# A two-layer MetaFormer on one core: the middle channel group laid out in alternating rows, and the next step's pieces at other places in the loop

## The chip, the core and the metric

The kernel runs on one core of a Trainium2 chip. The core has a matrix engine (TensorE, PE in the profile), a vector engine (VectorE, DVE), an activation engine (ScalarE, ACT), a general engine (GpSimd, POOL) and a queue that issues DMAs (SyncE, SP). Each engine works through its own list of instructions in order; semaphores tie the lists together. The metric is the time of one launch in microseconds; the kernel before took 13006.98 us, the median of three runs (13003.53 to 13008.28).

## What is computed

The input is two images of 96 channels, 128 by 128. Layer 0 is a four-direction selective scan (Mamba) and a feed-forward block, layer 1 a 3x3 convolution and a feed-forward block. Nearly all the time goes into the scan. Cut to that:

```python
def _mamba(x, in_w, conv_w, conv_b, xproj_w, dt_w, dt_b, A_log, Dp, outp_w):
    xc, z = jnp.split(x @ in_w.T, 2, axis=-1)                   # 192 channels each
    xc = silu(causal_conv(xc, conv_w, taps=4) + conv_b)
    xdbl = xc @ xproj_w.T
    dt_raw, Bm, Cm = xdbl[..., :6], xdbl[..., 6:22], xdbl[..., 22:]   # 16 states
    dt = softplus(dt_raw @ dt_w.T + dt_b)
    A = -exp(A_log)
    h = 0
    for t in range(L):                                          # L = 16384
        h = exp(dt[t, :, None] * A) * h + dt[t, :, None] * Bm[t] * xc[t, :, None]
        y[t] = (h * Cm[t]).sum(-1)
    return ((y + Dp * xc) * silu(z)) @ outp_w.T
```

It runs in four directions (rows, rows reversed, columns, columns reversed); the four results are joined, multiplied by `fuse_w` and added to the input.

## The kernel before

For each image, `normalize` writes the normalised image to DRAM by rows (`xnr`) and by columns (`xnc`), `mamba` does the scan, and `ffn_and_conv` the rest.

`mamba` takes the directions in two pairs, rows with columns, then both reversed. A pair has 2 x 192 = 384 channels, held as three groups of 128 partitions: group 0 is channels 0 to 127 of the first direction, group 2 is channels 64 to 191 of the second, and the middle group is mixed: its lower 64 partitions are channels 128 to 191 of the first direction and its upper 64 are channels 0 to 63 of the second. The time axis is cut into 32 tiles of T = 512, which makes 64 steps for an image, 128 in all.

A step has 24 units: 3 groups x 8 pairs of states. A loop turn k is one unit, and its main instructions are:

- POOL, `b_part` (L324): the row of B, spread over the partitions, times dt·u; two units ahead.
- ACT, `decay` (L330): two activations write exp(dt·A) into the PSUM tile `da`, of which there are three; two units ahead.
- DVE, `scan` (L334): two scans, one for each state, in place in `da`.
- In `behind`, one unit later: DVE multiplies the states by the row of C (L409), ACT copies the last column to `hst` (L410), and PE adds the two products into `y` by an identity matmul (`sums`, L341). At a group's end, which comes up in turn 1, 9 and 17 of a step, DVE multiplies y by the gate (`gated`, L349), and PE opens the next y with the `dmat` matmul (L416). There is one buffer for y.

The rows of B and C reach the partitions through DRAM. `rows_out` copies the 64 rows of a step to SBUF and writes them to the DRAM tile `bcd`, in four copies and by four DMAs (L261). `row_tile` (L320) reads a quad of states back, broadcast over the partitions: one DMA for groups 0 and 2, and for the middle group one for each 64 partitions, since the two halves belong to different directions. The buffers hold four quads of B and three of C; a C buffer is free when PE's `sums` has read it.

Everything of the next step that comes before its scan is cut into pieces and laid between the units of the running step (`prologue`; the list `at`). Each entry is (turn, where, piece); where = 0 comes at the start of a turn, before the scans, and where = 1 at its end, after `feed_decay`. The pieces are `load` (xa, xb), the `conv` of each group (the four taps folded into the weights, PE, L207) and its `conv_out` (ACT, L233), `gate` (PE, L207) and `gate_out` (ACT, L241), two `silu` over all three groups with an activation table load on either side (L244, L245), `rows`, and for each group the chain dt_in to dt_u (PE, ACT, POOL). Their PSUM results, and that of the output projection `project`/`collect` (L357 to L365, laid 4 turns behind a group's end), share the single buffer `misc`. The program order is the order on each engine:

```python
                issue(k, 0)
                ...
                    scan(i, g, s, 0, da, b, hs[k])
                if 0 < k <= total:
                    behind(k - 1)
                ...
                feed_decay(k + AHEAD)
                issue(k, 1)
```

In the middle group, `inproj` issues two matmuls for each tap: 64 output columns from xa to the lower half of the PSUM tile, 64 from xb to the upper half.

Of the kernel before, what the change touches and what calls it, by code (L numbers as in the profile page):

```python
# [10 lines left out]
F32 = mybir.dt.float32  # L11
# [4 lines left out]
ALU = mybir.AluOpType  # L16
# [16 lines left out]
COPIES = 4  # L33
# [4 lines left out]
BCO = 32  # L38
NBC = 4 * S
# [3 lines left out]
def tile_metaformer(ctx: ExitStack, tc: tile.TileContext, a: dict, out: bass.AP):  # L43
    nc = tc.nc

    cpool = ctx.enter_context(tc.tile_pool(name="const", bufs=1))
# [19 lines left out]
    inz = const("inz", (C, 4, DI))  # L66
# [11 lines left out]
    inx = cpool.tile([C, 4, 4, DI], F32, name="inx")  # L78
    nc.vector.memset(gmat, 0.0)
    with tc.tile_pool(name="prep", bufs=1) as pp, tc.tile_pool(name="prep_ps", bufs=2, space=PSUM) as pps:  # L80
        alog = pp.tile([128, 2, NG, S], F32, name="alog")
        nc.sync.dma_start(alog, a["alog"])
        nc.scalar.activation(alog, alog, AF.Exp)
        nc.vector.tensor_scalar_mul(amat, alog, -1.0)

        dskip = pp.tile([128, 2, NG], F32, name="dskip")
        nc.sync.dma_start(dskip, a["dskip"])
        for pi in range(2):
            for g in range(NG):
                nc.vector.tensor_scalar_mul(dmat[:, pi, g, :], ident, dskip[:, pi, g : g + 1])  # L90

        inxw = pp.tile([C, 4, DI], F32, name="inxw")
        nc.sync.dma_start(inxw, a["inx"])
        taps = pp.tile([C, 4, 4, DI], F32, name="taps")
        nc.sync.dma_start(taps, a["taps"].broadcast_to((C, 4, 4, DI)))
        for d in range(4):
            nc.vector.tensor_tensor(inx[:, d], taps[:, d], inxw[:, d, None, :].broadcast_to((C, 4, DI)), ALU.mult)
        outw = pp.tile([C, 4, DI], F32, name="outw")
        nc.sync.dma_start(outw, a["outw"])
        fusew = pp.tile([C, 4, C], F32, name="fusew")  # L100
        nc.sync.dma_start(fusew, a["fusew"])
        for pi, (da, db) in enumerate(PAIRS):

            pieces = [
                (slice(0, 128), da, 0, 128),
                (slice(0, 64), da, 128, 192),
                (slice(64, 128), db, 0, 64),
                (slice(0, 128), db, 64, 192),
            ]
            for g, (rows, d, lo, hi) in enumerate(pieces):  # L110
                ps = pps.tile([128, C], F32, name="ps")
                nc.tensor.matmul(ps[rows, :], outw[:, d, lo:hi], fusew[:, d, :], start=True, stop=True)
                nc.vector.tensor_copy(gmat[rows, pi, g, :], ps[rows, :])

    def layernorm(x, eps, dst, wp, psp, bufs=2, **cast):

# [66 lines left out]
    def mamba(acc, xnr, xnc):  # L183

        with ExitStack() as st:
# [3 lines left out]
            rows_d = pool("rows_d", 3, space=DRAM)  # L189
# [4 lines left out]
            def misc():  # L194
                return ps_m.tile([128, T], F32, name="misc")

            def inproj(pi, g, w, src, taps):

                ps = misc()
                for k in taps:  # L200
                    se = {"start": k == taps[0], "stop": k == taps[-1]}
                    for d, rows, lo, hi in (
                        ((0, slice(0, 128), 0, 128),),
                        ((0, slice(0, 64), 128, 192), (1, slice(64, 128), 0, 64)),
                        ((1, slice(0, 128), 64, 192),),
                    )[g]:
                        nc.tensor.matmul(ps[rows, :], w(PAIRS[pi][d], k, lo, hi), src[d][:, k : k + T], **se)  # L207
                return ps

            def prologue(pi, i, d):  # L210

                rev = pi == 1
                lo = L - (i + 1) * T if rev else i * T
                src = []
# [10 lines left out]
                    d["dt"], d["dtu"], d["yg"] = [], [], []  # L225

                def conv(g):
                    d["ps"] = inproj(pi, g, lambda dd, k, lo, hi: inx[:, dd, k, lo:hi], src, (0, 1, 2, 3))

                def conv_out(g):  # L230
                    if g == 0:
# [1 line left out]
                    nc.scalar.activation(d["xc"][:, g, :], d["ps"], AF.Identity, bias=convb[:, pi, g : g + 1])  # L233

                def gate(g):
                    d["ps"] = inproj(pi, g, lambda dd, k, lo, hi: inz[:, dd, lo:hi], src, (3,))

                def gate_out(g):
                    if g == 0:
# [82 lines left out]

            def b_part(d, g, b):
# [242 lines left out]
def _layout(v):  # L566

    f = np.float32
    order = [d for pair in PAIRS for d in pair]
    rows = lambda w: w[order].reshape(2, NG, 128, -1).transpose(2, 0, 1, 3)  # L570
# [11 lines left out]
    grouped = lambda w: w.reshape(2, NG, 128, -1).transpose(2, 0, 1, 3)  # L582
    out = {
        "x": v["x"].reshape(NB, C, L),
        "ident": np.eye(128, dtype=f),
        "inx": v["L0_conv_in_w"][:, :DI].transpose(2, 0, 1),
        "inz": v["L0_conv_in_w"][:, DI:].transpose(2, 0, 1),
        "taps": v["L0_conv_conv_w"].transpose(0, 2, 1)[None],
        "convb": rows(v["L0_conv_conv_b"])[..., 0],
        "bcw": grouped(bcw),  # L590
        "dtw": dtw,
        "dtb": rows(v["L0_conv_dt_b"])[..., 0],
        "alog": rows(v["L0_conv_A_log"]),
        "dskip": rows(v["L0_conv_Dp"])[..., 0],
        "outw": v["L0_conv_outp_w"].transpose(1, 0, 2),
        "fusew": v["L0_conv_fuse_w"].reshape(C, 4, C).transpose(2, 1, 0),
        "fuseb": v["L0_conv_fuse_b"].reshape(C, 1),
        "kw": v["L1_conv_kernel"].transpose(1, 2, 3, 0).reshape(C, 9, C),
    }
# [23 lines left out]
```

## Time and profile before

| What | us |
|---|---|
| median of the runs | 13006.98 |
| the profiled execution, its run | 13004.29 |
| its span | 13002.5 |
| DVE busy in it | 11569.1 |
| of that, scans (L334) | 7339.4 |
| of that, products with C (L409) | 3705.9 |
| PE busy, as modelled | 10850.3 |
| POOL busy | 9215.4 |
| ACT busy | 8560.0 |

A line of a timeline reads: start, duration, engine, line, operation, output<-inputs with their shapes, the number of instructions merged into it, and in brackets the idle time before it with what ended that. A line of the waits reads: engine, tile and line that waited, what it waited for, then the total in us, the number of times and the longest. An engine may stand idle at no cost if it isn't the one that sets the pace, so a wait counts where it delays the engine that does.

### The profile page before, as it was taken

What the parts mean: (1) busy time and instruction counts of PE and PEld (TensorE: products, weight loads), DVE (VectorE), ACT (ScalarE), POOL (GpSimd) and SP (SyncE); (2) the same over time, 40 slices, a digit from 0 to 9 for tenths busy, and PEclk for the clock granted to TensorE, in tenths of its full rate; (3) what the DMA queues carried; (4) which work ended last, traced back from release to release, by engine and by line L of the source; (5) the groups of instructions that cost most, each with busy time, mean ns of one, the idle gap of its engine ahead of it and who ended that gap; (6) DMA issues with size and microseconds to landing.
All of it is one profiled execution on the core that took longest, in us unless ns stands there. A gap on an engine that the chain in (4) does not pass through costs nothing. (4 is left out here: it accounts for less than half of the span.)

```text
span 13002.5 us, 97992 instructions
## 1 busy us (share of the span) xinstructions
PE 10850.3 (83%) x24208; PEld 3987.1 (31%) x24208; DVE 11569.1 (89%) x10865; ACT 8560.0 (66%) x14738; POOL 9215.4 (71%) x4772
## 2 busy tenths in 40 slices
PE   6888888888888888888978888888888888888889
PEld 2323233333333333333323333332333333333233
DVE  5999999999999999995459999999999999999954
ACT  6666666666666666665566666666666666666655
POOL 4877778777787787772147778777787777877721
PEclk8999999999999999999989999999999999999999
DMA  7999999999999999992079999999999999999920
GB/s 226 287 294 282 298 288 285 295 283 298 288 285 295 283 295 289 285 295 68 13 226 285 298 283 292 290 285 298 285 291 291 284 298 286 290 294 281 296 61 13
DMA packets 545331, 3400.40 MB, mean 262 GB/s; under 512 B 81612, under 2 KB 82732, under 8 KB 146840
## 3 DMA queue, kind: packets, MB, share of 16 engines
q1 hardware_dynamic: 544760, 3394.12, 83.1%
q8 instruction: 195, 3.19, 0.1%
q14 instruction: 376, 3.08, 0.1%
HBM read 3288.94 MB, written 104.86 MB: 261 GB/s over the span
## 5 line engine op out<-in xcount | busy, mean ns | idle before, releaser
L324 POOL TENSOR_TENSOR row<-dtu,row 128x1024 f32<-128x1024 f32 x3072 | 7175.7, 2358 | 1739.3 <-DMA row<-bcd 1419.2
L334 DVE TENSOR_TENSOR_SCAN da<-da,hst,row 128x512 f32<-128x512 f32 x5952 | 7339.4, 1274 | 351.2 <-ACT da L330 194.6
L341 PE MATMUL y<-row,ident 128*128 128x512 f32 x12288 | 6120.1, 626 | 1113.3 <-DVE row L409 1098.9
L330 ACT ACTIVATE da<-dt,amat 128x512 f32<-128x512 f32 x6144 | 4249.4, 692 | 207.5 <-ACT hst L410 0.4
L341 PEld LDWEIGHTS y<-row,ident 128*128 128x128 f32 x12288 | 2288.9, 197 | 4779.4 <-DVE row L409 2292.3
L409 DVE TENSOR_TENSOR row<-da,row 128x1024 f32<-128x1024 f32 x3072 | 3705.9, 1206 | 19.6 <-DMA row<-bcd 18.8
L410 ACT COPY hst<-da 128x2 f32<-128x2 f32 x3072 | 484.0, 158 | 2235.5 <-DVE row L409 2233.3
L416 PE MATMUL y<-xc,dmat 128*128 128x512 f32 x768 | 526.1, 773 | 779.1 <-DVE sz L349 779.1
L287 POOL TENSOR_TENSOR q<-e,q 128x512 f32<-128x512 f32 x384 | 488.0, 1271 | 821.8 <-ACT hst L410 709.1
L233 ACT ACTIVATE xc<-misc,convb 128x512 f32<-128x512 f32 x384 | 264.2, 688 | 1117.5 <-PE misc L207 1117.5
L207 PE MATMUL misc<-xa,inx 96*128 96x512 f32 (+1 forms) x2048 | 932.4, 597 | 59.0 <-DMA xa<-xnr 57.2
L207 PE MATMUL misc<-xb,inx 96*64 96x512 f32 (+1 forms) x2048 | 928.1, 595 | 1.6 <-ACT xc L233 1.6
L531 POOL TENSOR_TENSOR acc<-acc,y 96x512 f32<-96x512 f32 x128 | 147.6, 1153 | 987.0 <-DVE y L530 987.0
L541 PE MATMUL pc<-pad,kw 96*96 96x512 f32 x1152 | 566.7, 593 | 0.0
L207 PEld LDWEIGHTS misc<-xa,inx 96*128 96x128 f32 (+1 forms) x2048 | 323.6, 163 | 625.5 <-issue 493.4
L293 POOL TENSOR_TENSOR dt<-dt,ln 128x512 f32<-128x512 f32 x384 | 486.9, 1268 | 30.1
L297 POOL TENSOR_TENSOR dtu<-dt,xc 128x512 f32<-128x512 f32 x384 | 488.5, 1272 | 0.5
L290 POOL TENSOR_TENSOR ln<-ln,q 128x512 f32<-128x512 f32 x384 | 488.1, 1271 | 0.5
L359 PE MATMUL misc<-sz,gmat 128*96 128x512 f32 x1024 | 483.6, 594 | 0.0
L416 PEld LDWEIGHTS y<-xc,dmat 128*128 128x128 f32 x768 | 129.0, 211 | 1102.1 <-DVE sz L349 1099.1
L268 PE MATMUL misc<-rows,dtw 12*128 12x512 f32 x768 | 439.7, 652 | 18.5 <-ACT dt L275 17.2
L132 DVE TENSOR_TENSOR xq<-xm,rs 96x512 fp8e5<-96x512 f32 x128 | 87.9, 687 | 387.8 <-ACT rs L128 387.8
(75 smaller groups left out, 8403.8 us busy)
## 6 DMA issues: line engine op xcount, KB each, us to landing
row<-bcd SPq DMA_DIRECT2D x2048, 1024.0 KB, 7.5
row<-bcd SPq DMA_DIRECT2D x2048, 512.0 KB, 8.0
bcd<-rows SPq DMA_DIRECT2D x512, 128.0 KB, 9.8
xa<-xnr SPq DMA_DIRECT2D x124, 193.1 KB, 5.8
xb<-xnc SPq DMA_DIRECT2D x124, 193.1 KB, 5.5
acc<-in_x_dram SPq DMA_DIRECT2D x16, 768.0 KB, 17.8
xnr<-xn SPq DMA_DIRECT2D x16, 768.0 KB, 4.3
xnc<-stg SPq DMA_DIRECT2D x16, 768.0 KB, 5.6
```

Source lines behind the costliest of these rows:

```text
L207: nc.tensor.matmul(ps[rows, :], w(PAIRS[pi][d], k, lo, hi), src[d][:, k : k + T], **se)
L287: nc.gpsimd.tensor_tensor(d["q"], d["e"], d["q"], ALU.subtract)
L290: nc.gpsimd.tensor_tensor(d["ln"], d["ln"], d["q"], ALU.add)
L293: nc.gpsimd.tensor_tensor(d["dt"][g], d["dt"][g], d["ln"], ALU.add)
L297: nc.gpsimd.tensor_tensor(dtu, d["dt"][g], d["xc"][:, g, :], ALU.mult)
L324: nc.gpsimd.tensor_tensor(b, d["dtu"][g][:, None, :].broadcast_to((128, 2, T)), b, ALU.mult)
L330: nc.scalar.activation(da[:, j, :], d["dt"][g], AF.Exp, scale=amat[:, pi, g, s + j : s + j + 1])
L334: nc.vector.tensor_tensor_scan(h[:, j, :], da[:, j, :], b[:, j, :], 0.0 if i == 0 else hst[:, g, s + j : s + j + 1], ALU.mult, ALU.add,)
L341: nc.tensor.matmul(y, ident, c[:, j, :], start=False, stop=s + j == S - 1)
L409: nc.vector.tensor_tensor(c, h, c, ALU.mult)
L416: nc.tensor.matmul(y, dmat[:, pi, g, :], d["xc"][:, g, :], start=True, stop=False)
L541: nc.tensor.matmul(pc, kw[:, t, :], rows, start=t == 0, stop=t == 8)
```

## The change

The channels of the middle group are put in turn: even partitions hold the first direction, odd partitions the second. The weights are laid out on the host for this, with zeros in the rows (columns of the stationary operand) that belong to the other direction, so that every matmul of the middle group fills all 128 partitions: for each tap one from xa and one from xb are added into the same PSUM tile. `bcd` is written as two DMAs (B and C), each of which writes all four copies, and a quad of rows for the middle group is read by one DMA over all partitions, like those of the other groups. The order of the channels in `convb`, `bcw`, `dtw`, `dtb`, `alog`, `dskip` follows (`perm`). At the start, the taps are multiplied in one tap at a time through one buffer. The pieces of the next step stand at other turns.

```diff
-        taps = pp.tile([C, 4, 4, DI], F32, name="taps")
-        nc.sync.dma_start(taps, a["taps"].broadcast_to((C, 4, 4, DI)))
-        for d in range(4):
-            nc.vector.tensor_tensor(inx[:, d], taps[:, d], inxw[:, d, None, :].broadcast_to((C, 4, DI)), ALU.mult)
...
+        for k in range(4):
+            taps = pp.tile([C, 2, NG + 1, 128], F32, name="taps")
+            nc.sync.dma_start(taps, a["taps"][:, k].broadcast_to((C, 2, NG + 1, 128)))
+            nc.vector.tensor_tensor(inx[:, k], taps, inxw, ALU.mult)
...
-            def inproj(pi, g, w, src, taps):
+            def inproj(g, w, src, taps):
 
                 ps = misc()
-                for k in taps:
-                    se = {"start": k == taps[0], "stop": k == taps[-1]}
-                    for d, rows, lo, hi in (
-                        ((0, slice(0, 128), 0, 128),),
-                        ((0, slice(0, 64), 128, 192), (1, slice(64, 128), 0, 64)),
-                        ((1, slice(0, 128), 64, 192),),
-                    )[g]:
-                        nc.tensor.matmul(ps[rows, :], w(PAIRS[pi][d], k, lo, hi), src[d][:, k : k + T], **se)
+                parts = [(k, j) for k in taps for j in ((0,), (1, 2), (3,))[g]]
+                for n, (k, j) in enumerate(parts):
+                    nc.tensor.matmul(ps, w(k, j), src[j // 2][:, k : k + T], start=n == 0, stop=n == len(parts) - 1)
                 return ps
...
                 def rows_out():
-
                     d["rows"] = one.tile([BCO + NBC, T], F32, name="rows")
                     nc.scalar.copy(d["rows"], d["ps"][0 : BCO + NBC, :])
-                    d["bcd"] = rows_d.tile([COPIES, 2, NBC // 2, T], F32, name="bcd")
-                    for n in range(COPIES):
-                        nc.sync.dma_start(d["bcd"][n].rearrange("k r t -> (k r) t"), d["rows"][BCO:, :])
+
+                def rows_to_dram():
+
+                    d["bcd"] = rows_d.tile([2, COPIES, NBC // 2, T], F32, name="bcd")
+                    for k in range(2):
+                        r = d["rows"][BCO + k * NBC // 2 : BCO + (k + 1) * NBC // 2, None, :]
+                        r = r.broadcast_to((NBC // 2, COPIES, T))
+                        nc.sync.dma_start(d["bcd"][k].rearrange("n r t -> r n t"), r)
...
-                at = [(0, 0, load), (8, 1, partial(silu, "xc")), (14, 1, partial(silu, "sz"))]
-                at += [(12, 0, rows), (12, 1, rows_out)]
-                for g, k in enumerate((4, 5, 6)):
-                    at += [(k, 0, partial(conv, g)), (k, 1, partial(conv_out, g))]
-                for g, k in enumerate((7, 10, 11)):
-                    at += [(k, 0, partial(gate, g)), (k, 1, partial(gate_out, g))]
-                for g, k in enumerate((13, 18, 21)):
-                    pieces = (0, 0, dt_in), (0, 1, dt_exp), (1, 1, dt_ln), (2, 0, dt_q), (3, 0, dt_log), (3, 0, dt_sum), (4, 0, dt_u)
+                at = [(0, 0, load), (7, 1, partial(silu, "xc")), (12, 1, partial(silu, "sz"))]
+                at += [(12, 1, rows), (13, 0, rows_out), (13, 1, rows_to_dram)]
+                for g, k in enumerate((2, 4, 6)):
+                    at += [(k, 0, partial(conv, g)), (k + 1, 0, partial(conv_out, g))]
+                for g, k in enumerate((9, 10, 11)):
+                    at += [(k, 1, partial(gate, g)), (k + 1, 0, partial(gate_out, g))]
+                for g, k in enumerate((14, 17, 20)):
+                    pieces = (0, 1, dt_in), (1, 0, dt_exp), (1, 1, dt_ln), (3, 0, dt_q), (4, 0, dt_log), (4, 0, dt_sum), (5, 0, dt_u)
                     at += [(k + m, where, partial(f, g)) for m, where, f in pieces]
...
             def row_tile(d, g, s, k, ahead):
 
                 t = gen.tile([128, 4, T], F32, name=f"row{k}", bufs=ahead + 1)
-                for half in range(2) if g == 1 else (slice(None),):
-                    rows = slice(half * 64, half * 64 + 64) if g == 1 else half
-                    at = s + S * (half if g == 1 else g // 2)
-                    n = (64 if g == 1 else 128) // COPIES
-                    src = d["bcd"][None, :, k, at : at + 4, :].broadcast_to((n, COPIES, 4, T))
-                    nc.sync.dma_start(t[rows], src)
+
+                rows, nd = d["bcd"][k].rearrange("n (d s) t -> n d s t", d=2)[:, :, s : s + 4, :], 2
+                if g != 1:
+                    rows, nd = rows[:, g // 2 : g // 2 + 1], 1
+                src = rows.rearrange("n d s t -> (n d) s t")[None].broadcast_to((128 // nd // COPIES, nd * COPIES, 4, T))
+                nc.sync.dma_start(t, src)
                 return t
...
+    def padded(w):
+
+        t = np.zeros((w.shape[0], 2, NG + 1, 128), f)
+        for pi, (p, q) in enumerate(PAIRS):
+            t[:, pi, 0] = w[:, p, :128]
+            t[:, pi, 1, 0::2] = w[:, p, 128:]
+            t[:, pi, 2, 1::2] = w[:, q, :64]
+            t[:, pi, 3] = w[:, q, 64:]
+        return t
+
```

More of the change, by code (lines that the diff above doesn't have):

```diff
@@ L65, in tile_metaformer @@
     nc.vector.tensor_scalar_add(center, ident[0:C, 0:C], -1.0 / C)
-    inz = const("inz", (C, 4, DI))
+    inz = const("inz", (C, 2, NG + 1, 128))
     convb = const("convb", (128, 2, NG))
@@ L77, in tile_metaformer @@
     gmat = cpool.tile([128, 2, NG + 1, C], F32, name="gmat")
-    inx = cpool.tile([C, 4, 4, DI], F32, name="inx")
-    nc.vector.memset(gmat, 0.0)
+    inx = cpool.tile([C, 4, 2, NG + 1, 128], F32, name="inx")
     with tc.tile_pool(name="prep", bufs=1) as pp, tc.tile_pool(name="prep_ps", bufs=2, space=PSUM) as pps:
@@ L90, in tile_metaformer @@
                 nc.vector.tensor_scalar_mul(dmat[:, pi, g, :], ident, dskip[:, pi, g : g + 1])
-        inxw = pp.tile([C, 4, DI], F32, name="inxw")
+        inxw = pp.tile([C, 2, NG + 1, 128], F32, name="inxw")
         nc.sync.dma_start(inxw, a["inx"])
-        taps = pp.tile([C, 4, 4, DI], F32, name="taps")
-        nc.sync.dma_start(taps, a["taps"].broadcast_to((C, 4, 4, DI)))
-        for d in range(4):
-            nc.vector.tensor_tensor(inx[:, d], taps[:, d], inxw[:, d, None, :].broadcast_to((C, 4, DI)), ALU.mult)
-        outw = pp.tile([C, 4, DI], F32, name="outw")
-        nc.sync.dma_start(outw, a["outw"])
+        for k in range(4):
+            taps = pp.tile([C, 2, NG + 1, 128], F32, name="taps")
+            nc.sync.dma_start(taps, a["taps"][:, k].broadcast_to((C, 2, NG + 1, 128)))
+            nc.vector.tensor_tensor(inx[:, k], taps, inxw, ALU.mult)
+        outx = pp.tile([C, 2, NG + 1, 128], F32, name="outx")
+        nc.sync.dma_start(outx, a["outx"])
         fusew = pp.tile([C, 4, C], F32, name="fusew")
         nc.sync.dma_start(fusew, a["fusew"])
[L102 to L110, printed above, removed]
+        for pi, pair in enumerate(PAIRS):
+            for g in range(NG + 1):
                 ps = pps.tile([128, C], F32, name="ps")
-                nc.tensor.matmul(ps[rows, :], outw[:, d, lo:hi], fusew[:, d, :], start=True, stop=True)
-                nc.vector.tensor_copy(gmat[rows, pi, g, :], ps[rows, :])
+                nc.tensor.matmul(ps, outx[:, pi, g, :], fusew[:, pair[g // 2], :], start=True, stop=True)
+                nc.vector.tensor_copy(gmat[:, pi, g, :], ps)
     def layernorm(x, eps, dst, wp, psp, bufs=2, **cast):
@@ L227, in conv @@
                 def conv(g):
-                    d["ps"] = inproj(pi, g, lambda dd, k, lo, hi: inx[:, dd, k, lo:hi], src, (0, 1, 2, 3))
+                    d["ps"] = inproj(g, lambda k, j: inx[:, k, pi, j, :], src, (0, 1, 2, 3))
                 def conv_out(g):
@@ L235, in gate @@
                 def gate(g):
-                    d["ps"] = inproj(pi, g, lambda dd, k, lo, hi: inz[:, dd, lo:hi], src, (3,))
+                    d["ps"] = inproj(g, lambda k, j: inz[:, pi, j, :], src, (3,))
                 def gate_out(g):
@@ L569, in _layout @@
     order = [d for pair in PAIRS for d in pair]
-    rows = lambda w: w[order].reshape(2, NG, 128, -1).transpose(2, 0, 1, 3)
+    perm = np.arange(2 * DI)
+    perm[128:256] = perm[128:256].reshape(2, 64).T.reshape(-1)
+    grouped = lambda w: w.reshape(2, NG, 128, -1).transpose(2, 0, 1, 3)
+    rows = lambda w: grouped(w[order].reshape(2, 2 * DI, -1)[:, perm])
     xw = v["L0_conv_xproj_w"]
@@ L581, in _layout @@
             dtw[k * RK : (k + 1) * RK, pi, at] = v["L0_conv_dt_w"][d].T
-    grouped = lambda w: w.reshape(2, NG, 128, -1).transpose(2, 0, 1, 3)
+    def padded(w):
[6 more added lines that the diff above has]
+        return t
     out = {
@@ L585, in _layout @@
         "ident": np.eye(128, dtype=f),
-        "inx": v["L0_conv_in_w"][:, :DI].transpose(2, 0, 1),
-        "inz": v["L0_conv_in_w"][:, DI:].transpose(2, 0, 1),
-        "taps": v["L0_conv_conv_w"].transpose(0, 2, 1)[None],
+        "inx": padded(v["L0_conv_in_w"][:, :DI].transpose(2, 0, 1)),
+        "inz": padded(v["L0_conv_in_w"][:, DI:].transpose(2, 0, 1)),
+        "taps": padded(v["L0_conv_conv_w"].transpose(2, 0, 1))[None],
         "convb": rows(v["L0_conv_conv_b"])[..., 0],
-        "bcw": grouped(bcw),
-        "dtw": dtw,
+        "bcw": grouped(bcw[:, perm]),
+        "dtw": dtw[:, :, perm],
         "dtb": rows(v["L0_conv_dt_b"])[..., 0],
@@ L594, in _layout @@
         "dskip": rows(v["L0_conv_Dp"])[..., 0],
-        "outw": v["L0_conv_outp_w"].transpose(1, 0, 2),
+        "outx": padded(v["L0_conv_outp_w"].transpose(1, 0, 2)),
         "fusew": v["L0_conv_fuse_w"].reshape(C, 4, C).transpose(2, 1, 0),
```

## The prediction

> **What bounds the kernel now.** I read the page's busy times first, then who waited for whom in the scan stage of the first image (300 to 6000 us), then the timeline of one step, engine by engine.
>
> ```profile
> PE 10850.3 (83%) x24208; PEld 3987.1 (31%) x24208; DVE 11569.1 (89%) x10865; ACT 8560.0 (66%) x14738; POOL 9215.4 (71%) x4772
> ...
> DMA  7999999999999999992079999999999999999920
> ...
> row<-bcd SPq DMA_DIRECT2D x2048, 1024.0 KB, 7.5
> row<-bcd SPq DMA_DIRECT2D x2048, 512.0 KB, 8.0
> ```
>
> DVE leads, and the DMA engines look full. The last two lines say that half a quad of rows takes as long to land as a whole one. But who waits for it?
>
> ```profile
> POOL row L324 <- DMA row<-bcd: 702.6, 162, 7.1
> ...
> DVE da L334 <- ACT da L330: 98.1, 61, 1.9
> DVE sz L349 <- PE y L341: 82.8, 62, 2.1
> ...
> DVE da L334 <- ACT hst L410: 68.9, 60, 1.6
> ...
> DVE row L409 <- DMA row<-bcd: 9.2, 13, 2.1
> ```
>
> POOL waits for rows; DVE hardly does (9 us in 62 steps). DVE's waits come about once a step each, from ACT and PE. One step of 24 units in DVE's timeline: L349 runs at 1973.19, 2005.49, 2035.37 and 2063.86, so the groups take 32.3, 29.9 and 28.5 us. The third has no idle row and is the floor: 8 units of 3.487 us plus 0.6 for L349. Over all steps the first group takes 31.5 (69 times) or 32.3 (55 times), the others the same; the mean step is 31.86 + 29.9 + 28.5 = 90.26, of which 4.8 us is waiting. All 128 steps together wait some 610 us (4.7%), and that is all the change can win there.
>
> Where the first wait comes from:
>
> ```profile
> 1990.42 0.64 PE L207 MATMUL misc<-xa,inx 96*64 96x512 f32 x1
> 1990.43 0.64 PE L207 MATMUL misc<-xb,inx 96*64 96x512 f32 x1
> 1990.90 0.59 PE L207 MATMUL misc<-xa,inx 96*64 96x512 f32 x1
> 1990.91 0.59 PE L207 MATMUL misc<-xb,inx 96*64 96x512 f32 x1
> ...
> 1995.83 3.60 PE L207 MATMUL misc<-xb,inx 96*128 96x512 f32 x8
> ```
>
> ```profile
> 1999.47 0.69 ACT L233 ACTIVATE xc<-misc,convb 128x512 f32<-128x512 f32 x1 [3.16 <-PE misc L207]
> 2000.06 0.15 ACT L410 COPY hst<-da 128x2 f32<-128x2 f32 x1
> 2000.24 1.41 ACT L330 ACTIVATE da<-dt,amat 128x512 f32<-128x512 f32 x2
> ```
>
> ```profile
> 2001.76 1.29 DVE L334 TENSOR_TENSOR_SCAN da<-da,hst,row 128x512 f32<-128x512 f32 x1 [1.75 <-ACT da L330]
> 2002.96 1.21 DVE L409 TENSOR_TENSOR row<-da,row 128x1024 f32<-128x1024 f32 x1
> 2005.49 0.69 DVE L349 TENSOR_TENSOR sz<-y,sz 128x512 f32<-128x512 f32 x1 [1.33 <-PE y L341]
> ```
>
> The three convs crowd PE, conv_out stands in ACT's order waiting for them, and hst and da behind it come late; the scan starts 0.11 us after da ends. From conv_out's start to the scan is 2.29 us. Note the pairs: in the middle group the xa and xb matmuls, 64 columns each, start 0.01 us apart, so 16 passes take the time of 8 (a float32 matmul is two passes, 0.43 us apart).
>
> The rates and the PE clock (columns: stretch, busy times, then clock, DMA share, GB/s):
>
> ```profile
> 1994.00:2020.00 26.00, 24.93 (x59) 9.58 (x58) 22.51 (x20) 17.97 (x30) 13.00 (x6) 1.00 0.95 223
> 2020.00:2060.00 40.00, 29.26 (x58) 10.26 (x58) 38.84 (x35) 32.05 (x55) 32.99 (x18) 0.96 0.95 352
> ```
>
> ```profile
> 1974.00:1977.00 3.00, 3.00 (x5) 0.70 0.97 309
> ...
> 2064.50:2067.50 3.00, 2.84 (x6) 1.00 0.92 341
> ```
>
> At the same DMA share the half transfers get 223 GB/s, the whole ones 352. The last two lines open two successive steps: one has PE at a reduced clock, the other not; that is the 32.3 against the 31.5.
>
> [...]
>
> **The change part by part.**
>
> *Row DMAs.* 8 fewer issues a step (0.53 us each on SP) and the middle group at the full rate: 8 MB a step at 352 instead of 223 GB/s, 24 instead of 38 us. POOL's 11 us a step of waiting mostly goes. DVE gains only its own DMA waits, 18.8 us in all, and those sat in front of the ACT wait that follows: I take 0. bcd is written by two DMAs instead of four, the same bytes; on SP it now waits for rows_out behind the silu of sz, and the B fetch of unit 14 stands behind it; it is issued by then, took 9.8 us to land and is read at unit 18, 14 us later: 0. Next late on that path: nothing.
>
> *Full-width conv and gate of the middle group.* The pairs are gone: conv(1) is 16 passes in a row, 6.88 us instead of 3.44; gate(1) 1.72 instead of 0.86. PE has 4.3 us more a step in all; on average there is room (PE issues 156 passes, 67 us of 90), but not in the first group.
>
> *The pieces' new units.* As queue order: (k, after the decays) and (k+1, before them) are neighbours on ACT, so conv_out still comes directly behind da of its conv's unit + 2. conv moves from units 4,5,6 to 2,4,6; the silu of xc one unit earlier, 7; the gates to 10,11,12 on PE; the silu of sz from 14 to 12, away from dt_ln. I walk the first group with a full PE clock, time 0 at the L349 that opens it. DVE undisturbed starts unit 7's scan at 19.2 (1992.40 against 1973.19).
> PE in order: dmat and sums of unit 0 from 0.7 to 3.4, conv(0) to 6.85, sums(1) to 8.6, project (6 passes) to 11.2, sums(2) to 12.9, conv(1) to 19.75. conv_out(0) ends by 7.5 and collect by 12.3, so the one misc buffer is never late; xa, issued at 2058.79 and 5.8 us in landing, is there 2.7 us before conv(0) asks for it (2063.86 + 3.4). conv_out(1) starts at 12.87 + 7.07 = 19.95 (7.07: the 3.64 from an 8-pass conv's start to its conv_out, plus 8 × 0.43), the scan 2.29 later, 22.2: **a stall of 3.0**. Behind conv_out(1) on ACT stand hst(4) and da(7), and DVE waits for these.
> sums(3), sums(4), conv(2) begins at 23.2; conv_out(2) at 26.8; scan 9 may start at 29.1, DVE wants it at 22.2 + 6.97 = 29.2: no stall. sums(5) to (7) end at 32.0; L349 is wanted at 29.2 + 2.3 = 31.5: stall 0.5. First group **32.0** against 31.5 before.
> The silu of xc (4.10 with its two table loads) now stands before da(10): scan 10 at 26.8 + 8.0 = 34.8, wanted at 33.8: stall 1.05. The silu of sz behind gate_out(2) ends so that da(15) is ready at the very time its scan is wanted: 0 (cost if I am off: the same tenths). So the second group is 28.5 + 1.05 = **29.55** against 29.9; the 1.06 to 1.27 wait of before at unit 17 is gone. C rows for units 8 and 9 wait for sums(3), some 8 us later than undisturbed; with 5.1 us to land for a whole quad in the fast stretch they are there some 4 us early.
> Sum with a full clock: 32.0 + 29.55 + 28.5 = 90.05. With the reduced clock at the step's start, sums(0) and the first conv passes take 0.85 instead of 0.43: four passes, +1.6, all in front of conv(1), so all on DVE: 91.65. Before, that cost only 0.8. The clock in the changed kernel is what the trace can't show; I bound it by never (90.05) and always (91.65) and take every second step, as before: 90.85, +0.59 over 90.26, times 126 overlapped steps **+74 us**.
>
> *Preparation.* Four taps DMAs share one buffer, each waiting for the multiply that reads the last; the x loads stand behind them on SP. A 324 KB load lands in 3.5 us, a multiply of 1024 columns takes 1.2: x is asked for at some 22 instead of 6.8 us, of which about 15 was covered (the first normalize matmul starts at 22.6): +8. The first step of each image isn't overlapped: conv(1) and gate(1) cost it 4.3, less one DMA pair's issue, 1.2: 2 × 3.1 = +6. Together **+15** (bounds 5 and 25).
>
> Sum: 13004.3 (the profiled execution; span 13002.5) + 74 + 15 = 13093; the median shown is 13007, 0.02% off; I say 13090.
>
> **Rivals.**
> *A, the forecast, 13090, chance 0.42* (own range 13040 to 13150).
> *B, not slower: the clock stays up, 12990.* Place: the start of each step. [...] Then the step is 90.05, 0.21 below before: −26 + 15. [...] It decides if fewer than 6 steps in 100 start slow ((90.26 − 0.12 − 90.05) / 1.6). Its own range is 12870 to 13030, with a walk too long by up to 1 us a step. Chance 0.33.
> *C, faster: the rows are the bound, 12550.* If ACT's and PE's lateness hung on the half transfers, the first group would lose its stalls but the silu's: −3.75 × 126 + 15. For: DMA share 0.95 at 223 GB/s exactly in this stretch. Against: the scan follows da by 0.11 us, and ACT and PE wait for each other there, not for rows. Chance 0.10.
> *D, slower still, 13190.* Every step starts slow: 1.39 × 126 + 15 = 190; up to 13240 if da(15) misses too. Chance 0.15.
> That the middle group's rows don't get the full rate is no rival for the time: nothing on DVE's path hangs on it.
>
> **How the numbers follow.** A measurement of this kernel tells 0.2% (26 us) from no change. A: 0.38 slower, 0.04 same. B: 0.04 slower, 0.13 same, 0.16 faster. C faster, D slower. Slower 0.57, same 0.17, faster 0.26. The range leaves out C and the top of D: 12870 to 13240; A's own range stands above.
>
> **What would show it.** Right: L349 after L349 some 32 to 33.6, 29.6 and 28.5 us; the scan of unit 7 waiting 3 to 4.6 us for da behind a conv_out that waits for 16 single passes; no wait at unit 17; row landings near 5 us and POOL's DMA wait mostly gone without DVE noticing. Wrong: a first group under 31, xa and xb passes closer than 0.43, or DVE waits put down to rows.

## The result and the profile after

The changed kernel took 13569.01 us (median of four runs, 13559.2 to 13581.34) against 13007.63 us for the kernel before on the same chip (median of four): the ratio is 1.0431, 95% interval 1.0413 to 1.0449. The forecast had the direction right and missed the size: 13090 was said, and the time lies 329 us beyond the top of the range. The profiled execution took 13559.2 us, its span is 13557.4.

On the page of the kernel after (busy times, DMA share in 40 slices, then three groups with busy time, mean ns and the idle time before them, and the landing of a row transfer):

```profile
PE 11214.4 (83%) x24208; PEld 4294.5 (32%) x24208; DVE 11600.4 (86%) x10864; ACT 8541.3 (63%) x14738; POOL 9213.0 (68%) x4772
...
DMA  7888888889888888882078888889888898888820
...
L316 POOL TENSOR_TENSOR row<-dtu,row 128x1024 f32<-128x1024 f32 x3072 | 7176.7, 2354 | 3009.1 <-DMA row<-bcd 2307.0
L326 DVE TENSOR_TENSOR_SCAN da<-da,hst,row 128x512 f32<-128x512 f32 x5952 | 7376.2, 1284 | 695.0 <-ACT hst L402 510.7
...
L401 DVE TENSOR_TENSOR row<-da,row 128x1024 f32<-128x1024 f32 x3072 | 3741.0, 1218 | 311.5 <-DMA row<-bcd 307.6
...
row<-bcd SPq DMA_DIRECT2D x3072, 1024.0 KB, 9.3
```

DVE is as busy as before (11600 against 11569 us), so the loss is waiting. Two DVE lines carry it. L326, the scan, waits for ACT behind the late convolution: that was forecast. L401, the product with C (L409 before), waits 307.6 us for rows where the forecast had nothing; the kernel before had 18.8 us there. And a row transfer lands in 9.3 us, where the forecast looked for some 5.

The waits of the kernel after in the first image's scan stage (300 to 6000 us; total, times, longest) say the same, and show the queue behind them:

```profile
SPq L312 <- PE y L333: 2519.3, 724, 12.5
...
POOL row L316 <- DMA row<-bcd: 1112.0, 299, 12.2
...
DVE da L326 <- ACT hst L402: 251.0, 60, 5.0
...
DVE row L401 <- DMA row<-bcd: 146.9, 121, 3.2
```

That stretch holds 60 steps: the scan waits once a step, the product with C twice. DVE's own list is the ruler: from one `gated` (L349 before, L341 after) to the next is one group. Means over the first image's steps, in us:

| kernel | first group | second (middle) | third | step |
|---|---|---|---|---|
| before | 31.86 | 29.91 | 28.48 | 90.26 |
| after | 33.57 | 32.24 | 28.74 | 94.55 |
| forecast for after | 32.8 | 29.55 | 28.5 | 90.85 |

128 steps times 4.29 us are 549 of the 554.9 us by which the two profiled runs differ. Against the forecast the second group is off by 2.69 us a step (344 us), the first by 0.77 (99 us), the third by 0.24 (31 us).

One step after, the lines of DVE's timeline with idle time in brackets:

```profile
2080.49 1.29 DVE L326 TENSOR_TENSOR_SCAN da<-da,hst,row 128x512 f32<-128x512 f32 x1 [3.77 <-ACT hst L402]
2090.22 0.69 DVE L341 TENSOR_TENSOR sz<-y,sz 128x512 f32<-128x512 f32 x1 [0.36 <-PE y L333]
2093.06 1.29 DVE L326 TENSOR_TENSOR_SCAN da<-da,hst,row 128x512 f32<-128x512 f32 x1 [0.94 <-issue]
2106.63 1.22 DVE L401 TENSOR_TENSOR row<-da,row 128x1024 f32<-128x1024 f32 x1 [1.81 <-DMA row<-bcd]
2114.03 1.23 DVE L401 TENSOR_TENSOR row<-da,row 128x1024 f32<-128x1024 f32 x1 [0.32 <-DMA row<-bcd]
```

The first three are the forecast's own stalls (3.0 for conv_out(1), 0.5 at the gate, 1.05 for the silu). The last two, at the products of units 12 and 14, were not in it. In the first line the profile names `hst`, which came last; ACT's timeline shows what the scan of unit 7 needs, its decays, which end at 2080.39, 0.10 us before it starts, behind a conv_out that waited for PE:

```profile
2078.20 0.69 ACT L221 ACTIVATE xc<-misc,convb 128x512 f32<-128x512 f32 x1 [6.07 <-PE misc L195]
...
2078.97 1.42 ACT L322 ACTIVATE da<-dt,amat 128x512 f32<-128x512 f32 x2
```

The same stretch in windows (stretch, its length, busy time of PE, PEld, DVE, ACT and POOL, then clock, DMA share and GB/s):

```profile
2028.00:2032.00 4.00, 2.34 (x6) 1.06 (x6) 4.00 (x5) 1.54 (x3) 3.69 (x3) 1.00 1.02 424
...
2072.00:2076.00 4.00, 4.00 (x11) 1.84 (x10) 4.00 (x5) 0.13 (x1) 3.56 (x2) 1.00 0.86 184
2076.00:2080.00 4.00, 4.00 (x11) 1.75 (x10) 0.72 (x1) 1.74 (x4) 3.12 (x2) 1.00 0.00 0
2080.00:2084.00 4.00, 4.00 (x10) 1.71 (x9) 3.51 (x4) 1.86 (x4) 1.55 (x1) 1.00 0.68 156
2084.00:2088.00 4.00, 4.00 (x11) 1.82 (x10) 4.00 (x5) 2.85 (x5) 0.00 (x0) 1.00 1.04 223
2088.00:2092.00 4.00, 3.21 (x9) 1.19 (x8) 3.64 (x4) 3.93 (x5) 0.00 (x0) 1.00 1.02 219
...
2096.00:2100.00 4.00, 4.00 (x11) 1.66 (x10) 4.00 (x4) 1.78 (x5) 1.01 (x1) 1.00 1.06 229
```

At the end of conv(1) on PE (2071 to 2078 us), and for some us after it, the DMA engines stand still: the C buffer is free when PE's sums have read it, and SP, which works in order, waits for that with everything behind it (2519.3 us in the waits above). From 2084 they are fully busy (a share of 1.02 to 1.06 in the lines above), but at some 220 GB/s, the rate of the half transfers before (223). One transfer over all 128 partitions does not run at the rate of the others (the first line, from the third group of the step before: 424 GB/s). And they don't catch up: POOL stands still from 2084 to 2092, and DVE is held at 2106.

### The profile page after: what moved, and what is told of

It reads as the page before. It is cut to its first block, busy times and chain, and to the rows that moved or that the text cites. A ratio compares the mean times of both kernels' runs of the same rounds, so it can differ in the third digit from the quotient of the medians.

```text
span 13557.4 us, 95305 instructions
## 1 busy us (share of the span) xinstructions
PE 11214.4 (83%) x24208; PEld 4294.5 (32%) x24208; DVE 11600.4 (86%) x10864; ACT 8541.3 (63%) x14738; POOL 9213.0 (68%) x4772
## 5 line engine op out<-in xcount | busy, mean ns | idle before, releaser
L326 DVE TENSOR_TENSOR_SCAN da<-da,hst,row 128x512 f32<-128x512 f32 x5952 | 7376.2, 1284 | 695.0 <-ACT hst L402 510.7
L401 DVE TENSOR_TENSOR row<-da,row 128x1024 f32<-128x1024 f32 x3072 | 3741.0, 1218 | 311.5 <-DMA row<-bcd 307.6
L333 PEld LDWEIGHTS y<-row,ident 128*128 128x128 f32 x12288 | 2252.4, 194 | 5110.0 <-DVE row L401 2857.8
L195 PE MATMUL misc<-xa,inx 96*128 96x512 f32 x2048 | 999.4, 600 | 58.8 <-DMA xnc<-stg 57.0
L195 PE MATMUL misc<-xb,inx 96*128 96x512 f32 x2048 | 983.5, 592 | 1.6 <-ACT xc L221 1.6
L408 PE MATMUL y<-xc,dmat 128*128 128x512 f32 x768 | 459.3, 682 | 618.7 <-DVE sz L341 618.7
L265 ACT ACTIVATE e<-misc,dtb 128x512 f32<-128x512 f32 x384 | 263.8, 687 | 693.5 <-PE misc L260 667.0
L195 PEld LDWEIGHTS misc<-xa,inx 96*128 96x128 f32 x2048 | 401.2, 196 | 586.5 <-issue 541.1
L195 PEld LDWEIGHTS misc<-xb,inx 96*128 96x128 f32 x2048 | 386.4, 189 | 494.8 <-issue 491.6
L229 ACT COPY sz<-misc 128x512 f32<-128x512 f32 x384 | 224.7, 585 | 376.5 <-PE misc L195 376.5
```

The source lines that it names most:

```text
L195: nc.tensor.matmul(ps, w(k, j), src[j // 2][:, k : k + T], start=n == 0, stop=n == len(parts) - 1)
L326: nc.vector.tensor_tensor_scan(h[:, j, :], da[:, j, :], b[:, j, :], 0.0 if i == 0 else hst[:, g, s + j : s + j + 1], ALU.mult, ALU.add,)
L333: nc.tensor.matmul(y, ident, c[:, j, :], start=False, stop=s + j == S - 1)
L401: nc.vector.tensor_tensor(c, h, c, ALU.mult)
```

## The experiments

The theory: the middle group's transfers are slow because of their shape, 16 repeats of 8 runs, where the other groups' have 32 repeats of 4 (a run is a quad's rows in one copy, 8 KB; the runs are read in turn, one for each partition, and then repeated for the next partitions); and the DMA engines were so nearly full that this, together with the other parts, holds the second group. The rival: the second group is late because PE is, whatever the rows do. own16, copies8, after_old_at, half_conv and half_conv_rows32 were run once each; the kernels with four runs or more spread over 2 to 26 us, so a few tens of us between single runs say little.

**The shape of the transfer.** rows32 reads the middle group from two of the four copies, so that it also has 32 repeats of 4:

```diff
-                rows, nd = d["bcd"][k].rearrange("n (d s) t -> n d s t", d=2)[:, :, s : s + 4, :], 2
-                if g != 1:
-                    rows, nd = rows[:, g // 2 : g // 2 + 1], 1
-                src = rows.rearrange("n d s t -> (n d) s t")[None].broadcast_to((128 // nd // COPIES, nd * COPIES, 4, T))
+                rows = d["bcd"][k].rearrange("n (d s) t -> n d s t", d=2)[:, :, s : s + 4, :]
+                rows = rows[:, g // 2 : g // 2 + 1] if g != 1 else rows[0 : COPIES // 2]
+                src = rows.rearrange("n d s t -> (n d) s t")[None].broadcast_to((32, 4, 4, T))
```

> The changed kernel with one edit: a quad of rows for the middle group is read as 32 repeats of 4 sources (two copies of each direction) instead of 16 repeats of 8 sources. Theory 1 (the slow rate, 220 GB/s in the changed kernel's middle-group stretch, comes from how 16 repeats of 8 partitions fall on the DMA engines and SBUF): the stretch runs at 350 GB/s or more, DVE's waits for rows fall from 308 us to under 40, the second group takes 29.6 instead of some 32.3 us, 13240 us in all. Theory 2 (reading two directions at once from DRAM is slow): the rate stays near 220 and the time within 30 us of 13569.

rows32 took 13241.28 us, ratio to the kernel before 1.0184 (1.0168 to 1.0199): 328 us less than the changed kernel for this edit, as theory 1 had it. The groups are 33.48, 29.59 and 29.13. Its page:

```profile
DMA  6777777777777777772067777777777777777710
...
L400 DVE TENSOR_TENSOR row<-da,row 128x1024 f32<-128x1024 f32 x3072 | 3709.4, 1207 | 0.1
...
row<-bcd SPq DMA_DIRECT2D x3072, 1024.0 KB, 6.1
```

The product with C waits for nothing any more, and a row lands in 6.1 instead of 9.3 us. The windows of rows32 over the end of conv(1) in a step (one that starts at a reduced PE clock, 0.53 from 2100 to 2103 us):

```profile
2116.00:2120.00 4.00, 4.00 (x11) 1.83 (x10) 2.50 (x3) 0.00 (x0) 3.40 (x2) 1.00 0.00 0
2120.00:2124.00 4.00, 4.00 (x10) 1.71 (x9) 0.85 (x1) 3.00 (x7) 1.25 (x1) 1.00 0.11 18
2124.00:2128.00 4.00, 4.00 (x11) 1.74 (x10) 4.00 (x5) 0.85 (x2) 0.00 (x0) 1.00 0.94 369
...
2132.00:2136.00 4.00, 3.21 (x8) 1.19 (x8) 2.70 (x4) 3.87 (x7) 2.90 (x2) 1.00 1.01 424
```

The DMA engines stand still here too, and the first group is as long as before the edit (33.48 against 33.57), so PE's lateness is still there. Now they make it good at 369 to 424 GB/s.

own16 keeps the division into 16 x 8 but reads 16 different sources, each of them eight times in a row, instead of the same eight sources 16 times:

```diff
+                if g == 1:
+                    src = d["bcd"][k].rearrange("n (q r) t -> (n q) r t", r=4)[0:16, None].broadcast_to((16, 8, 4, T))
```

> The changed kernel with the middle group reading 16 different sources, each for 8 partitions in a row (the same bytes and shape in SBUF, but not the right rows of B and C). Theory A1 (the slow rate comes from the 8 neighbouring partitions [...]): it stays near 220 GB/s, 13569 us within 40. Theory A2 (it comes from all engines reading the same 8 sources in turn): 350 GB/s or more, some 13240 us.

13534.59 us, and 9.2 us to land: reading the same eight sources in turn isn't the cause. copies8 gives the shape to the other two groups instead, and 32 x 4 to the middle one:

```diff
-COPIES = 4
+COPIES = 8
...
+                rows = rows[:, g // 2 : g // 2 + 1] if g != 1 else rows[0:2]
+                src = rows.rearrange("n d s t -> (n d) s t")[None]
+                src = src.broadcast_to((16, 8, 4, T) if g != 1 else (32, 4, 4, T))
```

> The rows32 kernel with eight copies in DRAM instead of four: groups 0 and 2 now read 16 repeats of 8 sources of one direction, the middle group 32 repeats of 4. Theory A (16 repeats of 8 is slow whatever is read): groups 0 and 2 go at some 220 GB/s, a step is held by the rows at about 100 us, 14000 us or more. Theory B (reading two directions in turn is what is slow): groups 0 and 2 stay at 350 GB/s or more and the time within 60 us of 13240.

```profile
DMA  7999999999998989895079999999998999898940
...
L401 DVE TENSOR_TENSOR row<-da,row 128x1024 f32<-128x1024 f32 x3072 | 3711.6, 1208 | 966.5 <-DMA row<-bcd 964.0
...
row<-bcd SPq DMA_DIRECT2D x3072, 1024.0 KB, 14.1
```

15660.29 us. Two windows of a step, the first while rows of groups 0 and 2 move, the second with rows of the middle group:

```profile
2040.00:2050.00 10.00, 6.14 (x10) 1.74 (x9) 8.19 (x8) 3.57 (x8) 9.46 (x6) 0.81 1.02 237
...
2090.00:2100.00 10.00, 8.37 (x20) 3.35 (x19) 8.69 (x9) 7.21 (x13) 8.64 (x4) 1.00 1.04 360
```

The slow rate has moved to transfers that read one direction alone, and the mixed ones in 32 x 4 are quick. So the mixture of two directions isn't the cause either; it is the shape, 16 x 8 against 32 x 4. Which of its two numbers counts, the repeats or the runs, was not separated. The step takes 111.15 us here: DVE waits 7.5 us of it for rows, and 8.9 for the decays of the first group, behind a convolution whose xa takes 21.2 us to land (5.3 in the kernel after).

**The parts of the change, one at a time.** before_new_at is the kernel before with its pieces at the new units and nothing else:

```diff
-                at = [(0, 0, load), (8, 1, partial(silu, "xc")), (14, 1, partial(silu, "sz"))]
...
+                at = [(0, 0, load), (7, 1, partial(silu, "xc")), (12, 1, partial(silu, "sz"))]
+                at += [(12, 1, rows), (13, 0, rows_out), (13, 1, rows_to_dram)]
+                for g, k in enumerate((2, 4, 6)):
...
```

> The kernel before, with half transfers and paired matmuls, but with the changed kernel's units for the pieces. Theory 1 (the units are good, and the full-width conv is what costs the first group): no wait at unit 7, first group 28.6 (full PE clock) to 30.2, second 29.6 or somewhat more where the slow rows can't follow, 12600 to 12750 us. Theory 2 (the new units themselves are the loss): a wait for da at unit 7 stays, 13000 us or more.

13110.95 us, ratio 1.0082 (1.0065 to 1.0099): a miss of mine. The first group did gain (30.52 instead of 31.86), but the second gave back more (31.76 instead of 29.91). Its DVE line for the product with C shows where:

```profile
L411 DVE TENSOR_TENSOR row<-da,row 128x1024 f32<-128x1024 f32 x3072 | 3712.7, 1209 | 248.4 <-DMA row<-bcd 230.8
...
row<-bcd SPq DMA_DIRECT2D x2048, 512.0 KB, 8.9
```

With the new units the half transfers of the kernel before hold the second group. The kernel before was close to that edge already: in its scan stage the DMA share is 0.91 of a step of 90.26, 82 us. The share in before_new_at is 0.91 as well, so the mean doesn't show the difference. Which of the moved pieces used up the slack was not tried.

after_old_at is the converse, the changed kernel with the old units (the same two lists exchanged, the bcd write at turn 12).

> The changed kernel with the units of before. Theory 1 (the full-width conv costs PE 3.4 us in the first group wherever it stands): first group 35 us or more, 13700 to 13900 us. Theory 2 (the new units are the loss): 13300 us or less.

13415.2 us, between both expectations: the first group is 34.88, just under the 35 of theory 1, and the second 30.22; the product with C waits only 68.8 us for rows. With padded convolutions and slow rows the new units cost 154 us more than the old.

before_rows16 is the kernel before with the row transfers of the change alone, and before_rows32 the same in the fast form:

```diff
+                if g == 1:
+                    src = d["bcd"][k].rearrange("n (d s) t -> n d s t", d=2)[:, :, s : s + 4, :]
+                    src = src.rearrange("n d s t -> (n d) s t")[None].broadcast_to((16, 2 * COPIES, 4, T))
+                    nc.sync.dma_start(t, src)
```

> The kernel before with the change's row transfers alone: one transfer over 128 partitions (16 repeats of 8 runs) for each quad of B or C of the middle group, and two transfers into the copies; convolutions, gates and units as before. Half of the middle group's channels then meet the other direction's B and C, since its channels still stand in halves. Theory 1 (the row part by itself costs nothing on DVE's path, as predicted; its slow rate is that of the two halves before, 221 against 223 GB/s, and it hurt only where the sums came late): 12970 to 13050 us, second group 29.8 to 30.2. Theory 2 (the 16 x 8 transfers by themselves hold the second group): second group above 31, 13150 us or more.

> As before_rows16, in 32 repeats of 4 runs, the fast form. Theory 1 (the kernel before had its middle rows slow but on time, DVE waited 18.8 us for rows in all): no gain, 12960 to 13010 us. Theory 2 (rows already held the second group of the kernel before, 29.9 where 28.5 is possible): second group 29.4 or less, 12850 to 12930 us.

before_rows16: 13042.41 us, ratio 1.0033 (1.0020 to 1.0046), groups 31.89, 30.17, 28.48. before_rows32: 13001.61 us, ratio 0.9999 (0.9991 to 1.0008), groups 31.86, 29.89, 28.48. With the old units the slow form costs 39 us (DVE waits 96.9 us for rows instead of 18.8) and the fast form brings nothing. One transfer at the full rate in place of two is worth 0 by itself, as the forecast had it. The rate is worth more with the new units, as half_conv and rows32 show.

half_conv computes the middle group's convolution and gate from xa alone, 8 passes instead of 16, which is PE's time before; it leaves the second direction's channels of that group out:

```diff
-                parts = [(k, j) for k in taps for j in ((0,), (1, 2), (3,))[g]]
+                parts = [(k, j) for k in taps for j in ((0,), (1,), (3,))[g]]
```

> The changed kernel with the middle group's conv and gate taken from xa alone (the second direction's channels of that group are left out), so that conv(1) has 8 passes and gate(1) 2, as before in time. Theory 1 (PE's lag starts both losses: the wait at unit 7, and the late C rows behind it): first group 28.7 to 30.3, DVE's waits for rows under 100 us, 12600 to 12750 us. Rival (the rows are slow by themselves and hold the second group whatever PE does): second group still 31.5 or more, 13100 us or more.

13115.64 us. The first group falls to 30.17, the second stays at 32.30, as the rival had it, and the product with C waits for rows as long as in the kernel after:

```profile
L401 DVE TENSOR_TENSOR row<-da,row 128x1024 f32<-128x1024 f32 x3072 | 3713.2, 1209 | 309.3 <-DMA row<-bcd 303.2
```

Rows hold the second group with PE on time too, so PE's lateness isn't what makes them late. With both edits:

> Both edits at once: the rows as 32 repeats of 4 sources, and the middle group's conv and gate from xa alone (the second direction's channels of that group are left out). Theory 1 (two separate losses, PE's wait in the first group and the slow rows in the second): first group 30.2, second 29.6, third 28.5, some 12760 us. Rival (one loss hides behind the other, so that removing either gave most of it): 12950 us or more.

12801.35 us, with groups of 30.05, 29.57 and 29.13: theory 1, 41 us over its figure.

| | slow rows | fast rows | the rows' part |
|---|---|---|---|
| padded convolution | 13569 | 13241 | 328 |
| half of it | 13116 | 12801 | 314 |
| the convolution's part | 453 | 440 | |

The two losses add up: 768 us together, 781 taken one by one. 440 us are 3.4 us a step, which is conv(1)'s extra PE time (3.44 in the forecast), and all of it is in the first group (33.48 against 30.05).

So, half_conv standing for the pairs of before (its PE time is theirs, and with slow rows it comes within 5 us of before_new_at, which has the pairs): from before_rows32 the new units without the padding bring 200 us (13002 to 12801), the padding costs 440, the slow transfer 328. These are steps along one chain of kernels, so their sum, +568 against the +561 measured, is no test of them, and in another order the parts are others: with slow rows the new units bring nothing (13111 against 13000).

**A version that beats both.** Once the rows are fast, conv(1) could be paid for if nothing else stood in its group. spread takes rows32 and deals the pieces out over the step: conv at turns 2, 4 and 9, each `conv_out` further behind its conv, the gates at 15 to 20, and `project` up to 15 turns behind its group.

> The rows32 kernel with the pieces spread for a PE that has 16 passes for the middle conv: conv at turns 2, 4 and 9 with conv_out at 3, 7 and 10, the silu of xc at 11, the gates at 15, 18 and 20, the silu of sz at 23, and group 2's output projection at turn 14 instead of 3. Theory 1 (PE's overload of the first group is the whole of its loss): no wait over 0.5 us in a step, groups of 28.5 to 29 us, some 12450 us. Rival (something else holds the first group, POOL or the rows): a first group of 30 us or more, 12700 us or more.

13231.67 us, ratio 1.0179 (1.0162 to 1.0196), a miss. The first group is at the floor, 28.5 (theory 1), but the third went to 34.4. DVE's timeline of spread, between the `gated` that opens the third group and the one that ends it:

```profile
2062.18 0.69 DVE L341 TENSOR_TENSOR sz<-y,sz 128x512 f32<-128x512 f32 x1
2075.24 1.29 DVE L326 TENSOR_TENSOR_SCAN da<-da,hst,row 128x512 f32<-128x512 f32 x1 [0.72 <-ACT da L322]
2080.50 1.29 DVE L326 TENSOR_TENSOR_SCAN da<-da,hst,row 128x512 f32<-128x512 f32 x1 [1.65 <-issue]
2087.03 1.29 DVE L326 TENSOR_TENSOR_SCAN da<-da,hst,row 128x512 f32<-128x512 f32 x1 [2.92 <-ACT da L322]
2096.34 0.68 DVE L341 TENSOR_TENSOR sz<-y,sz 128x512 f32<-128x512 f32 x1
```

Three scans wait for decays (the second too: its da ends 0.08 us before it). ACT, which makes them, stands before the last two in a wait for the projection and for `dt_in`, which share the one `misc` buffer with the gates:

```profile
2078.24 0.68 ACT L355 ACTIVATE acc<-misc,fuseb 96x512 f32<-96x512 f32 x1 [3.09 <-PE misc L351]
...
2083.64 0.69 ACT L265 ACTIVATE e<-misc,dtb 128x512 f32<-128x512 f32 x1 [2.25 <-PE misc L260]
```

spread2 moves these apart (`rows` and `project` move by one to three turns too):

```diff
-                at = [(0, 0, load), (11, 1, partial(silu, "xc")), (23, 1, partial(silu, "sz"))]
+                at = [(0, 0, load), (12, 1, partial(silu, "xc")), (24, 1, partial(silu, "sz"))]
...
-                for g, k, out in ((0, (15, 0), (15, 1)), (1, (18, 1), (19, 0)), (2, (20, 0), (20, 1))):
+                for g, k, out in ((0, (13, 0), (13, 1)), (1, (17, 0), (17, 1)), (2, (23, 0), (23, 1))):
...
-                for g, k in enumerate((15, 17, 20)):
+                for g, k in enumerate((15, 18, 21)):
```

> As spread (rows of the middle group in 32 repeats, all pieces of the next step dealt out over the units of the step), but the pieces that need the shared scratch buffer and ScalarE at the third group (silu of the gate, the step sizes, the gate itself) stand further apart. Theory 1, the third group lost its 6 us in spread because its own pieces were crowded, ScalarE running the silus, the step sizes and the decays of one unit in a row, and not for want of an engine or of rows: every group stands between 28.4 and 29.5 us, 86 to 88 us a step, 12400 to 12600 us in all. Theory 2, ScalarE or the rows bound the step once the stalls are spread: the time moves from the third group to another, the step stays at 90 us or above, 12850 us or more.

12834.13 us, ratio 0.9870 (0.9853 to 0.9886): 1.3% quicker than the kernel before, with all of the computation and the padding in it. The groups are 28.79, 30.93 and 29.2, a step of 88.92. That lies between the expectations: 5 us of the third group went with the crowding, as theory 1 said, but 2.2 us of waiting now stand in the middle group, as theory 2 said. In the scan stage of spread2 (300 to 6000 us) two waits of DVE are left, and rows are not among them:

```profile
DVE da L326 <- ACT da L322: 117.8, 128, 2.1
DVE sz L341 <- PE y L333: 59.4, 63, 2.2
```

## Why the prediction was wrong

*The step that failed* is the end of "Row DMAs": "the middle group at the full rate", "Next late on that path: nothing", and with it the sentence under the rivals that "nothing on DVE's path hangs on it". Both halves failed. The rate was about 220 GB/s instead of the 352 that was put in, so by that rate the middle group's 8 MB still take some 38 us of a step and not 24. And DVE's path did hang on it: the product with C waits 307.6 us for rows, and 328 us went when the rate alone was mended (rows32). The forecast's 0 for DVE is right for the kernel before (before_rows32, 0.9999). It was wrong to carry that 0 over to other units. With the new ones DVE waits for rows even where the padding is left out (303.2 us, half_conv); with the padding and the old ones it waits 68.8 (after_old_at).

The walk did ask whether the C rows come late, but for units 8 and 9 only, the first quad of the middle group, and found them "some 4 us early" at 5.1 us for a landing. In the trace DVE waits for none of these. It waits at unit 12 (in 124 steps of 124, 211 us) and at unit 14 (in 121, 94 us), the third and fourth quads. The landings took 9.3 us and not 5.1, a delay can grow from quad to quad, and the walk stopped at the first.

*The rate.* That one transfer over all 128 partitions would run like the whole transfers of the kernel before (352 GB/s) was an estimate. It holds for the 32 x 4 form (424 GB/s in rows32). In the 16 x 8 form it was 223, with all 128 partitions written. The measurement decides: the span of partitions isn't enough. Why is open. The DMA share of 1.02 to 1.06 in the lines of the slow stretch is a mean over 16 engines, so all of them were busy; the trace does not show which engine wrote which partitions.

*Full-width conv and the walk of the first group* held. conv(1)'s 16 passes begin at 2071.13, and the sums behind them at 2078.00: 6.87 us, 6.88 forecast. Forecast and measured stalls: 3.0 and 3.77 at unit 7, 0.5 and 0.36 at the gate. The group is 32.8 or 34.5 us (66 and 58 steps) where 32.0 or 33.6 was said. (The 1.6 between the two forecasts is four passes at 0.85 us instead of 0.43: in the kernel before, five passes of `sums` from 1974.89 take 4.01 us, at a granted clock of 0.57, and four from 2065.56 take 1.88, at 1.00.) The walk was 0.8 to 0.9 us short, 99 us in all, because conv(1) begins 13.73 us after the `gated` that opens the group (2057.40) and not 12.87. The term is "project (6 passes)":

```profile
2065.98 1.88 PE L349 MATMUL misc<-acc,ident 96*96 96x512 f32 x2
2067.68 1.90 PE L351 MATMUL misc<-sz,gmat 128*96 128x512 f32 x4
...
2071.13 1.02 PE L195 MATMUL misc<-xa,inx 96*128 96x512 f32 x2
```

It takes 3.43 us, not 2.6. The two passes of L349 take 0.85 each here, where 0.43 was put in: they read `acc` for group 2 with a step of 128 elements from column to column. For group 1, with step 1, the same passes are 0.43 apart (two from 2035.30 take 1.02 us). The granted clock is 1.00 in both places.

*The silu of xc* costs 0.94 at the scan of unit 10, 1.05 forecast. With fast rows the second group is 29.59, forecast 29.55: there nothing but the rows was missing. *The third group* is 28.74 for 28.5.

*Preparation* was put at +15. What lies outside the stretch from the first to the last `gated` of each image grew by 2.4 us: the first came at 201.20 instead of 201.88, the gap between the images grew by 3.0, the end by 0.1. The 8 us for the taps did not show.

*The rivals.* B took the clock to stay up at the start of a step. In the kernel after it is 1.00 in the 3 us from 2058.00, behind the `gated` at 2057.40, and 0.63 in those from 2151.20, behind the one at 2150.61; what sets it was not shown. C named rows as the bound, with the right resource and the wrong sign: it took for granted that the change would make them quicker. D went further up, but for the clock. Rows that stay slow were considered and priced at nothing, although "DVE waits put down to rows" stood among the signs of a wrong forecast; that is the sign that came.

## What to carry to other kernels

That nobody waits for a resource says only that its slack covers the present order, and its mean share says little: the DMA share was 0.91 in the kernel before and in before_new_at, and DVE's waits for rows 18.8 and 230.8 us. When the order changes, follow the transfers of the busiest stretch to the last one before costing them at nothing. Take the rate of a transfer from a row of the same shape (repeats x runs), not from the number of partitions (223 and 424 GB/s here, over 128 partitions both). And where moved pieces share one buffer and one in-order engine, look where they stand next: here spread brought the first group to its floor and the third from 29.1 to 34.4 us.

## What the hardware showed beside that

A broadcast read of 1 MB to 128 partitions ran at 219 to 237 GB/s in the windows shown as 16 repeats of 8 runs, and at 360 to 424 as 32 repeats of 4 of the same size, with a DMA share of 1.02 to 1.06 in the first and 0.94 to 1.04 in the second. The writes of `bcd` took longer beside the slow form: 10.8 to 11.0 us to land in after, after_old_at, own16, half_conv and before_rows16, and 3.2 to 6.4 in the kernels in which all rows had the fast form.

A matmul pass of 96 x 512 float32 took 0.85 us with the moving operand read at a step of 128 elements and 0.43 at a step of 1, at a granted clock of 1.00 (L349 of the kernel after, from 2065.98 and from 2035.30).
